# The decoder's steps: biases kept in PSUM, three full products, and four matmuls of ones per step

## The chip, the cores and the metric

The kernel runs on one core of a Trainium2 chip. The metric is device time in microseconds (us) of one launch, lower is better. The engines are named as the profile names them: PE (TensorE's matmuls) and PEld (its weight loads), DVE (VectorE), ACT (ScalarE), POOL (GpSimd), SP (SyncE, which issues most DMAs).

## The reference, cut to what matters

The model is a chain of eight residual blocks on x (16 sequences of 64 tokens, 128 features, f32). The first is a recurrent decoder with attention; a mixture of experts (MoE) follows it, then a perceiver, a quantised MLP, six transformer layers, an MoE, a block and an MoE. Only the decoder and the seam to the first MoE are touched. For each of the 16 sequences the decoder computes, with its input row x normalised:

```
def step(carry, x):
    h, stopped = carry
    stop = jnp.logical_or(stopped, jnp.mean(x) == 0)
    logits = jnp.concatenate([x, h]) @ W_attn.T + b_attn
    aw = jax.nn.softmax(logits)
    applied = aw @ enc
    comb = jax.nn.relu(jnp.concatenate([x, applied]) @ W_comb.T + b_comb)
    h_new = jnp.tanh(comb @ W_ih.T + b_ih + h @ W_hh.T + b_hh)
    out = h_new @ W_out.T + b_out
    ...
```

The 64 steps depend on each other through h, which is 128 features by 16 sequences. Everything that hangs on x alone can be computed for all steps before.

## The kernel before, in words

The decoder is `decoder()`, called as the first of `STAGES`. It has three parts.

The part before the steps normalises x (`norm_half`), transposes it and the context to features (`to_features`), and computes for all steps at once what depends on x: XL, the attention logits of x with biases and mask (`wax2`), XC, minus the combined product with its bias (`wcx`), HX, the state's share of that (`wih`), and E2, the contexts times `wca`, each in SBUF.

The steps are written out in order (`manual_schedule`). In step t TensorE adds to the PSUM tile lg the product of `wah2` with h; ACT takes the exponential into bd (two sequences lie in one block of 128 partitions, so bd has 16 columns); `su` is the sum over a block by a matmul with ones, DVE takes its reciprocal r; `cb` is the context product, 8 blocks of 2 columns; DVE multiplies cb with r and takes the maximum with XC, which is the relu, into co; `hh` collects `whh` times h and `wih` times co; ACT takes tanh into H. lg and hh of the next step begin with a matmul of the identity with XL or HX, a copy into PSUM. `mm4` splits a product into four of 32 output rows each; with f32 every matmul runs as two passes, so `mm4` shows as 8 records and a full product as 2. A list `todo` (`exact_zero`) holds small DVE operations that test exactly whether the mean of a normalised row is zero; some are emitted at the end of each step.

The part after the steps builds `keep` (one until a row has stopped) with a matmul of `tri`, multiplies H with `wout`, adds the bias, masks, adds x, and reduces the reciprocals to their extremes (`watch`), which the end of the kernel checks. Then `moe("m0", ...)` begins, whose operations are ordered by a planner (`_Plan`): each has an engine, an assumed duration and its dependences. The planner also places `fill`: matmuls of ones in bf16 (`units`, 128x512) into a PSUM buffer that nobody reads.

All weights of the first stages are loaded at the start on SP's queue: x, the constants, the context, w0 (the decoder's), then m0 in 8 parts, m0_bd, w1 in 4 parts, wd. All matmuls but the transposes and those of other helpers have line 296 (`mm`) in the profile, so they are told apart by the names of their tiles.

Of the kernel before, what the change touches and what calls it, by code (L numbers as in the profile page):

```python
# [27 lines left out]
NEG = -1e30  # L28
# [14 lines left out]
def _cols(v):  # L43

    return v.reshape(-1, 128).T
# [60 lines left out]
def _layout(i):  # L106
# [7 lines left out]
    arrays["x"] = i["x"].reshape(NTOK, D)  # L114
    arrays["ctx"] = i["ctx_1024"].reshape(NTOK, D)
# [4 lines left out]
    for name, m in (("km_s", i["mask_BxS_bf0"]), ("km_c", i["mask_BxS2_bf0"])):  # L120
# [8 lines left out]
        ("wax", p["W_attn"][:, :D].T),  # L129
        ("wah", p["W_attn"][:, D:].T),  # L130
        ("wcx", p["W_comb"][:, :D].T),
        ("wca", p["W_comb"][:, D:].T),
# [3 lines left out]
        ("bcomb", _cols(p["b_comb"])),  # L136
        ("bih", _cols(p["b_ih"])),
        ("bhh", _cols(p["b_hh"])),
        ("battn", battn),
        ("wah2", np.tile(p["W_attn"][:, D:].T, (1, 2))),  # L140
        ("wax2", np.tile(p["W_attn"][:, :D].T, (1, 2))),
        ("battn2", np.tile(_cols2(p["b_attn"]), (2, 1))),
        ("bout", _rep(p["b_out"])),
# [81 lines left out]
class _Net:  # L225
    def __init__(self, ctx, tc, ins, at):
        self.tc, self.nc, self.ins, self.at = tc, tc.nc, ins, at
        self.const = ctx.enter_context(tc.tile_pool(name="const", bufs=1))
        self.wts = ctx.enter_context(tc.tile_pool(name="wts", bufs=1))
        self.xres = ctx.enter_context(tc.tile_pool(name="xres", bufs=2))  # L230
        self.small = ctx.enter_context(tc.tile_pool(name="small", bufs=2))
        self.n = 0
        nc = self.nc
        self.load_consts()
        self.x = self.xres.tile([128, NT, D], F32, tag="x", name="x_in")
        nc.sync.dma_start(out=self.x, in_=ins["x"].rearrange("(i p) d -> p i d", p=128))
# [18 lines left out]
    def load_consts(self):  # L255
# [6 lines left out]
        nc.sync.dma_start(out=self.ctx, in_=self.ins["ctx"].rearrange("(i p) d -> p i d", p=128))  # L262
# [1026 lines left out]
class _Fast(_Net):  # L1289
# [5 lines left out]
    def __init__(self, ctx, tc, ins, at):  # L1295
# [7 lines left out]
        rows = ins["x"].rearrange("(i p) d -> p i d", p=128)  # L1303
        for h in range(2):
            nc.sync.dma_start(out=self.x[:, h * 4:(h + 1) * 4, :], in_=rows[:, h * 4:(h + 1) * 4, :])

    def load_rest(self, first):
# [7 lines left out]
        nc.sync.dma_start(out=c[:, :cut], in_=src[:, :cut])  # L1315
        self.ctx = self.const.tile([128, NT, D], F32, tag="ctx", name="ctx_tok")
        nc.sync.dma_start(out=self.ctx, in_=self.ins["ctx"].rearrange("(i p) d -> p i d", p=128))
        self.w0 = self.load("w0", "w0", parts=2, pool=first)
# [15 lines left out]
    def mm4(self, out, lhsT, rhs, start=True, stop=True):  # L1334

        for k in range(4):
            rows = slice(32 * k, 32 * k + 32)
            self.mm(out[rows, :], lhsT[:, rows], rhs, start, stop)

    def watch(self, k, r):  # L1340

        nc = self.nc
        nc.vector.tensor_reduce(self.extremes[:, 0, k:k + 1], r, AX.X, ALU.max)
        nc.vector.tensor_reduce(self.extremes[:, 1, k:k + 1], r, AX.X, ALU.min)
# [23 lines left out]

    def load(self, name, tag, parts=1, layout=None, pool=None, bufs=None):
        if tag in ("moe", "moe_b2"):  # L1370
            pool = self.moew
        elif tag == "wd":
            pool = self.wide
        return super().load(name, tag, parts, layout, pool, bufs)
# [3 lines left out]
    def norm_half(self, x, h, out):  # L1378
# [7 lines left out]
        v, r = self.s([128, 4], "lh_v", 4), self.s([128, 4], "lh_r", 4)  # L1386
        nc.vector.tensor_scalar(v, mv[:, :, 1], EPS, None, ALU.add)
        nc.gpsimd.tensor_tensor(r, v, self.minus_half[:, 0:4], ALU.pow)
        nb = self.s([128, 4], "lh_nb", 4)
        nc.vector.scalar_tensor_tensor(nb, mv[:, :, 0], -1.0, r, ALU.mult, ALU.mult)  # L1390
        for k in range(4):
            if k % 2:
                nc.vector.tensor_scalar(
                    out[:, k, :], x[:, h * 4 + k, :], r[:, k:k + 1], nb[:, k:k + 1], ALU.mult, ALU.add)
            else:
                nc.scalar.activation(
                    out[:, k, :], x[:, h * 4 + k, :], AF.Identity, bias=nb[:, k:k + 1], scale=r[:, k:k + 1])
# [112 lines left out]
    def decoder(self):  # L1510
        nc, tc = self.nc, self.tc
        w = self.w0
        x = self.x
        with ExitStack() as st:
            pool = st.enter_context(tc.tile_pool(name="d_sb", bufs=1))
            full = lambda tag: self.tile(pool, [128, B, T], tag)
            H, lnT, XL, XC, HX, RR = (full(k) for k in ("H", "lnT", "XL", "XC", "HX", "RR"))
            E2 = self.tile(pool, [128, NT, D], "E2")
            keep, zero = self.tile(pool, [128, NT], "keep"), self.tile(pool, [128, NT], "zero")
            ones = self.tile(pool, [128, 128], "ones")  # L1520
            nc.gpsimd.memset(ones, 1.0)
            bsum, lbias = self.tile(pool, [128, 1], "bsum"), self.tile(pool, [128, B], "lbias")
            todo = self.exact_zero(pool, x, zero)
            with tc.tile_pool(name="d_ps", bufs=4, space=PSUM) as ps, tc.manual_schedule(engines=None):
                ln = self.tile(pool, [128, NT, D], "ln")
                flat = lambda a, h: a[:, h * 8:(h + 1) * 8, :].rearrange("p b t -> p (b t)")
                ctxT = full("ctxT")
                for h in range(2):
                    self.norm_half(x, h, ln[:, h * 4:(h + 1) * 4, :])
                self.to_features(ps, self.ctx, lambda h, t: nc.vector.tensor_copy(flat(ctxT, h), t))  # L1530
                self.to_features(ps, ln, lambda h, t: nc.scalar.copy(flat(lnT, h), t))

                nc.vector.tensor_scalar(lbias, self.c("half16"), -NEG, NEG, ALU.mult, ALU.add)
                nc.vector.tensor_scalar(lbias, lbias, w("battn2"), None, ALU.add)
                nc.vector.tensor_tensor(bsum, w("bih"), w("bhh"), ALU.add)
                for h in range(2):
                    t = self.tile(ps, [128, 512], "pj")
                    self.mm(t, w("wcx"), flat(lnT, h))
                    nc.vector.tensor_scalar(flat(XC, h), t, w("bcomb"), -1.0, ALU.add, ALU.mult)
                for h in range(2):  # L1540
                    t = self.tile(ps, [128, 512], "pj")
                    self.mm(t, w("wax2"), flat(lnT, h))
                    nc.vector.tensor_tensor(
                        XL[:, h * 8:(h + 1) * 8, :], t.rearrange("p (b t) -> p b t", t=T),
                        lbias[:, h * 8:(h + 1) * 8].unsqueeze(2).to_broadcast([128, 8, T]), ALU.add)
                for h in range(2):
                    t = self.tile(ps, [128, 512], "pj")
                    self.mm(t, w("wih"), flat(XC, h))
                    nc.scalar.activation(flat(HX, h), t, AF.Identity, bias=bsum, scale=-1.0)
                for h in range(2):  # L1550
                    t = self.tile(ps, [128, 4, 128], "pj")
                    for k in range(4):
                        i = h * 4 + k
                        self.mm(t[:, k, :], ctxT[:, 2 * i:2 * i + 2, :].rearrange("p b t -> p (b t)"), w("wca"))
                    self.evac(h, E2[:, h * 4:(h + 1) * 4, :], t)

            with tc.tile_pool(name="d_rs", bufs=2) as rp, tc.tile_pool(name="d_rps", bufs=2, space=PSUM) as ps, \
                    tc.manual_schedule(engines=None):
                for t in range(T):
                    h = w("cond") if t == 0 else H[:, :, t - 1]  # L1560
                    su, cb = (self.tile(ps, [128, 16], k) for k in ("su", "cb"))
                    if t == 0:
                        lg, hh = (self.tile(ps, [128, 16], k) for k in ("lg", "hh"))
                    if t == 0:
                        self.mm(lg, self.ident, XL[:, :, t], True, False)
                    self.mm4(lg, w("wah2"), h, False, True)
                    bd = self.tile(rp, [128, 16], "bd")
                    nc.scalar.activation(bd, lg, AF.Exp)  # L1568
                    if t == 0:
                        self.mm(hh, self.ident, HX[:, :, t], True, False)  # L1570
                    self.mm4(hh, w("whh"), h, False, False)
                    self.mm4(su, ones, bd)
                    r = RR[:, :, t]
                    nc.vector.reciprocal(r, su)
                    for c in range(NT):
                        self.mm4(cb[:, 2 * c:2 * c + 2], E2[:, c, :], bd[:, 2 * c:2 * c + 2])
                    if t < T - 1:
                        lg = self.tile(ps, [128, 16], "lg")
                        self.mm(lg, self.ident, XL[:, :, t + 1], True, False)
                    co = self.tile(rp, [128, 16], "co")  # L1580
# [951 lines left out]
```

## Time and profile before

| | |
|---|---|
| median of the runs shown | 1666.67 us (1665.7, 1666.67, 1673.75) |
| profiled execution: time, span | 1675.33 us, 1673.1 us |
| mean granted clock of TensorE | 0.904 |
| PE busy, PEld busy | 1501.8 us (90%), 1085.0 us (65%) |
| DVE, ACT, POOL busy | 779.8, 536.2, 185.6 us |
| decoder's first matmul of a step, its last tanh ends | 20.4 us, 225.1 us |
| granted clock from 28.25 to 225.1 us | 0.50 |
| first 128x512 matmul of the MoE | 239.2 us |

The ends of matmuls are modelled, so busy time of PE does not tell how much of the array works; the granted clock is what the throttle allowed, 1 being full speed. A row of the timeline gives start and length in us, the engine, the line, the operation, the tile written and those read, the shape, the number of records merged, and in brackets the idle time of the engine before it and what ended it.

### The profile page before, as it was taken

How to read it: one execution, taken by the hardware profiler on the slowest of the kernel's cores; microseconds unless marked ns; L12 is line 12 of the kernel's file. 1: busy time of each engine (PE TensorE's matmuls, PEld its weight loads, DVE VectorE, ACT ScalarE, POOL GpSimd, SP SyncE). 2: the span in 40 equal slices, each digit the busy share in tenths (PEclk: the TensorE clock that was granted, in tenths of full speed). 3: DMA queues.
4: the chain of work that ended last, by engine and by line, in shares of the span. 5: the costliest groups of instructions: out<-in, count | busy, mean ns of one | idle time of the engine just before them, and what ended most of it. 6: DMA issues, size and time to landing. Idle time of an engine off the chain costs nothing.

```text
span 1673.1 us, 51674 instructions
## 1 busy us (share of the span) xinstructions
PE 1501.8 (90%) x23514; PEld 1085.0 (65%) x23514; DVE 779.8 (47%) x2457; ACT 536.2 (32%) x885; POOL 185.6 (11%) x227
## 2 busy tenths in 40 slices
PE   6999989999995699889888989898999899999997
PEld 5888866665774256566655656555576677776665
DVE  3435351226435476565665656565311544345112
ACT  1111134433331123334342433334433233332431
POOL 0000010001000041222221222122000101001000
PEclk7555569999998789999999999999999999999998
DMA  6000000000000050100000000000300200000000
GB/s 223 4 4 5 4 2 1 0 1 2 3 2 10 0 189 17 30 12 12 26 21 16 13 20 12 21 2 2 139 2 1 103 3 2 3 3 1 1 1 16
DMA packets 14354, 38.74 MB, mean 23 GB/s; under 512 B 1682, under 2 KB 6674, under 8 KB 14125
## 3 DMA queue, kind: packets, MB, share of 16 engines
q1 hardware_dynamic: 14125, 35.34, 6.2%
q8 instruction: 186, 3.05, 0.8%
q14 instruction: 43, 0.35, 0.1%
HBM read 34.81 MB, written 0.52 MB: 21 GB/s over the span
## 4 chain that ended last, share of the span: by engine, by line
PE 82%; DVE 11%; ACT 3%; issue 2%; DMA 1%; POOL 0%; SPq 0%; ACTq 0%; DVEq 0%
PE pj L296 42%; PE y L296 11%; PE O L296 9%; PE S L296 6%; PE cb L296 3%; PE hh L296 3%; PE lg L296 3%; DVE qx L2371 2%; PE pj L1926 1%; DVE u L2321 1%; ACT P L2449 1%; PE su L296 1%; PE pj L2262 1%; ACT bd L1568 1%; DVE nq L2209 1%
## 5 line engine op out<-in xcount | busy, mean ns | idle before, releaser
L296 PEld LDWEIGHTS y<-m_sb,H 128*128 128x128 f32 x1568 | 188.7, 192 | 57.3 <-issue 35.6
L296 PE MATMUL y<-m_sb,H 128*128 128x128 f32 x1568 | 193.5, 276 | 16.9 <-DVE x L1732 9.8
L296 PE MATMUL pj<-xT,m_sb 128*128 128x512 f32 x392 | 182.3, 594 | 0.0
L2215 POOL TENSOR_TENSOR nq<-nq,minus_half 128x2 f32<-128x2 f32 x120 | 85.1, 714 | 605.2 <-DVE nq L2212 571.7
L2403 ACT ACTIVATE P<-S 128x1024 f32<-128x1024 f32 x96 | 98.0, 1021 | 116.9 <-PE S L296 116.9
L1708 ACT ACTIVATE H<-pj,m_sb 128x512 f32<-128x512 f32 x128 | 87.5, 687 | 132.7 <-PE pj L296 132.4
L1732 DVE SCALAR_TENSOR_TENSOR x<-y,cw,x 128x128 f32<-128x128 f32 x128 | 39.0, 346 | 186.8 <-PE y L296 186.8
L296 PEld LDWEIGHTS pj<-xT,m_sb 128*128 128x128 f32 x392 | 68.6, 191 | 57.4 <-issue 56.9
L2245 ACT ACTIVATE xn<-x,nq 128x128 f32<-128x128 f32 x100 | 48.4, 492 | 160.1 <-DVE nq L2218 150.3
L2321 DVE TENSOR_TENSOR u<-pj,consts_sb 128x512 f32<-128x512 f32 x96 | 66.3, 691 | 42.6 <-PE pj L296 42.4
L1838 DVE COPY QKV<-pj 128x512 f32<-128x512 f32 x56 | 38.7, 691 | 71.5 <-PE pj L296 71.4
L1708 ACT ACTIVATE H<-pj,b1g,m_sb 128x512 f32<-128x512 f32 x64 | 49.6, 778 | 58.5 <-PE pj L296 55.8
L296 PE MATMUL cb<-bd,E 128*32 128x2 f32 x4096 | 65.4, 192 | 3.2 <-issue 3.1
L296 PEld LDWEIGHTS cb<-bd,E 128*32 128x32 f32 x4096 | 62.8, 156 | 3.6 <-issue 3.2
L296 PE MATMUL pj<-xT,w_sb 128*128 128x512 f32 x128 | 63.1, 610 | 0.9 <-ACT G L2056 0.5
L296 PE MATMUL pj<-xT,l_f 128*128 128x512 f32 x96 | 51.3, 627 | 11.7 <-ACT P L2449 11.5
L296 PE MATMUL pj<-units 128*128 128x512 bf16 x195 | 57.9, 409 | 4.2 <-DVE x L2077 1.9
L1732 DVE SCALAR_TENSOR_TENSOR acc<-y,cw,acc 128x128 f32<-128x128 f32 x64 | 19.5, 346 | 86.5 <-PE y L296 86.5
L1584 ACT ACTIVATE H<-hh 128x16 f32<-128x16 f32 x64 | 12.9, 202 | 138.9 <-PE hh L296 138.9
L296 PE MATMUL pj<-xT,l_s 128*128 128x512 f32 x96 | 52.5, 663 | 5.5 <-DVE u L2321 2.8
L296 PEld LDWEIGHTS O<-Vs,P 128*64 128x64 f32 x1536 | 49.7, 140 | 10.8 <-issue 8.9
L296 PE MATMUL O<-Vs,P 128*64 128x18 f32 x1536 | 53.6, 214 | 3.1 <-DVE On L2416 3.0
(363 smaller groups left out, 2704.3 us busy)
## 6 DMA issues: line engine op xcount, KB each, us to landing
w_sb<-in_w SPq DMA_DIRECT2D x7, 681.5 KB, 8.3
m_sb<-in_m SPq DMA_DIRECT2D x8, 515.0 KB, 7.0
m_sb<-in_m SPq DMA_DIRECT2D x8, 514.5 KB, 6.0
m_sb<-in_m SPq DMA_DIRECT2D x7, 565.5 KB, 9.5
l_f<-in_l SPq DMA_DIRECT2D x6, 578.5 KB, 3.7
l_a<-in_l SPq DMA_DIRECT2D x6, 387.0 KB, 3.2
l_s<-in_l SPq DMA_DIRECT2D x6, 384.0 KB, 3.2
w_sb<-in_w SPq DMA_DIRECT2D x4, 512.5 KB, 11.8
```

The source lines that it names most:

```text
L296: self.nc.tensor.matmul(out, lhsT=lhsT, rhs=rhs, start=start, stop=stop, **kw)
L1568: nc.scalar.activation(bd, lg, AF.Exp)
L1708: nc.scalar.activation(a[:, c, :], ups[c].slot[1], act, bias=b, scale=g)
L1732: nc.vector.scalar_tensor_tensor(acc[:, k, :], src, g, x0[:, i, :] if first else acc[:, k, :], ALU.mult, ALU.add)
L1838: e(o, i.rearrange("p (b t) -> p b t", t=T) if len(o.shape) == 3 else i)
L1926: t = plan.op("PE", 700, lambda t, On=On: [nc.tensor.transpose(t[:, i * 128:(i + 1) * 128], On.slot[1][:, i * 128:(i + 1) * 128], self.ide ...
L2209: nc.vector.bn_stats(out=t[:, i, 0:6], in_=xk[:, i, :])
L2215: return lambda t: nc.gpsimd.tensor_tensor(t[:, :, b], t[:, :, a], self.minus_half[:, 0:2], ALU.pow)
L2245: nc.scalar.activation(o, xk[:, i, :], AF.Identity, bias=f[1], scale=f[0])
L2321: us.append(plan.op("DVE", 690, lambda u, t=t, k=k, table=table: nc.vector.tensor_tensor(view(u[:, k, :]), view(t.slot[1]), self.c(table). ...
L2371: nc.vector.tensor_scalar(o, r, m, None, ALU.mult)
L2403: P = plan.op("ACT", 1030, lambda P, S=S: nc.scalar.activation(P.rearrange("p (g c) -> p g c", g=4), S.slot[1][:, :, 0:256], AF.Exp, scale ...
```

## The change

The diff changes how the decoder starts, steps and ends.

Biases and logits: the PSUM banks lg and hh now hold all 64 steps (two banks each, 32 steps of 16 columns). Matmuls of the identity with broadcast biases fill them at the start, and the products of x are added into the banks in eight portions of 8 steps, logits(k) and states(k), portion 0 before or in step 0, portion t in steps 1 to 7. XL, HX and their identity matmuls per step are gone. states(k) uses `nwih`, minus `wih`.

The step: `wah2`, `whh` and `wih` are full products instead of `mm4`. bd has a second column of zeros per sequence, so cb has 4 columns per block, and one tensor_tensor_scan (multiply, then maximum) replaces multiply and maximum; the reciprocal is written beside XC. `fill` puts matmuls of ones into the idle one of the two su banks: one behind `whh`, one behind cb, two behind `wih`; in steps 1 to 7 logits(t) and states(t) stand in the place of two of them.

Loads: x and ctx come in another layout (one row of 4 KB a partition), ctx and the constants on ACT's queue; m0, m0_bd, w1 and wd are loaded in 14 portions in every third step from step 2 (`load_later`), each behind a copy on POOL that waits for that step's state.

The end: `keep` and `base` (x plus the masked bias) are made in steps 58 to 62, `watch` in steps 31, 59 and 63, and the output product becomes four quarters in the MoE's plan (`decoder_end`).

```diff
+    def load_later(self, name, tag, parts=1, pool=None):
...
+            def begin(gate, a=a, b=min(n, a + step)):
+                nc.gpsimd.tensor_copy(t[:, a:a + 1], gate[:rows])
+                nc.sync.dma_start(out=t[:, a:b], in_=src[:, a:b])
+
+            self.later.append(begin)
...
+            lgs, hhs, sus, cbs = ([self.tile(ps, [128, 512], f"{k}{i}") for i in range(2)]
+                                  for k in ("lg", "hh", "su", "cb"))
...
+            known = dict(start=False, stop=True, skip_group_check=True)
+            for k in range(2):
+                self.mm(lgs[k], self.ident, lbias.unsqueeze(1).to_broadcast([128, 32, B]))
+                self.mm(hhs[k], self.ident, bsum.unsqueeze(2).to_broadcast([128, 32, B]))
...
+            def logits(k):
+                self.mm(sums(lgs, k), w("wax2"), lnT[:, :, 8 * k:8 * k + 8].rearrange("p b t -> p t b"), **known)
+
+            def states(k):
+                self.mm(sums(hhs, k), nwih, XC[:, 8 * k:8 * k + 8, :, 1], **known)
...
-                    if t == 0:
-                        self.mm(lg, self.ident, XL[:, :, t], True, False)
-                    self.mm4(lg, w("wah2"), h, False, True)
-                    bd = self.tile(rp, [128, 16], "bd")
-                    nc.scalar.activation(bd, lg, AF.Exp)
-                    if t == 0:
-                        self.mm(hh, self.ident, HX[:, :, t], True, False)
-                    self.mm4(hh, w("whh"), h, False, False)
-                    self.mm4(su, ones, bd)
-                    r = RR[:, :, t]
-                    nc.vector.reciprocal(r, su)
-                    for c in range(NT):
-                        self.mm4(cb[:, 2 * c:2 * c + 2], E2[:, c, :], bd[:, 2 * c:2 * c + 2])
-                    if t < T - 1:
-                        lg = self.tile(ps, [128, 16], "lg")
-                        self.mm(lg, self.ident, XL[:, :, t + 1], True, False)
-                    co = self.tile(rp, [128, 16], "co")
-                    nc.vector.tensor_tensor(co, cb, r, ALU.mult)
-                    nc.vector.tensor_tensor(co, co, XC[:, :, t], ALU.max)
-                    self.mm4(hh, w("wih"), co, False, True)
-                    nc.scalar.activation(H[:, :, t], hh, AF.Tanh)
-                    if t < T - 1:
-                        hh = self.tile(ps, [128, 16], "hh")
-                        self.mm(hh, self.ident, HX[:, :, t + 1], True, False)
-                    for _ in range(-(-len(todo) // (T - t))):
+            for t in range(T):
+                h = w("cond") if t == 0 else H[:, :, t - 1]
+                lg, hh = (k[t // 32][:, (t % 32) * B:(t % 32 + 1) * B] for k in (lgs, hhs))
+                su, cb, bd = sus[t % 2], cbs[t % 2], bds[t % 2]
+                idle = sus[(t + 1) % 2]
+                self.mm(lg, w("wah2"), h, **known)
+                nc.scalar.activation(bd[:, :, 1], lg, AF.Exp)
+                if t > 0:
+                    self.mm(hh, w("whh"), h, **known)
+                self.fill(idle, 1)
+                self.mm4(su[:, :B], ones, bd[:, :, 1])
+                nc.vector.reciprocal(XC[:, t, :, 0], su[:, :B])
+                for c in range(NT):
+                    self.mm4(cb[:, 4 * c:4 * c + 4], E2[:, c, :],
+                             bd[:, 2 * c:2 * c + 2, :].rearrange("p b k -> p (b k)"))
+                if t == 0:
+                    states(0)
+                    self.mm(hh, w("whh"), h, **known)
+                elif t < 8:
+                    logits(t)
+                else:
+                    self.fill(idle, 1)
+                co = self.tile(rp, [128, B, 2], "co")
+                nc.vector.tensor_tensor_scan(
+                    co.rearrange("p b k -> p (b k)"), cb[:, :2 * B], XC[:, t, :, :].rearrange("p b k -> p (b k)"),
+                    0.0, ALU.mult, ALU.max)
+                self.mm(hh, w("wih"), co[:, :, 1], **known)
+                nc.scalar.activation(H[:, :, t], hh, AF.Tanh)
+                if 0 < t < 8:
+                    states(t)
+                self.fill(idle, 1 if 0 < t < 8 else 2)
+                if t % 3 == 2 and self.later:
+                    self.later.pop(0)(H[:, 0, t:t + 1])
+                if todo:
+                    for _ in range(-(-len(todo) // (T - 6 - t))):
                         todo.pop(0)()
...
+                elif t == T - 6:
+                    self.mm(su[:, 32:32 + NT], self.c("tri"), zero)
+                    nc.vector.tensor_scalar(keep, su[:, 32:32 + NT], 0.5, None, ALU.is_lt)
...
+                for k, (a, b) in enumerate(((0, 32), (32, 60), (60, T))):
+                    if t == b - 1:
+                        self.watch(3 + k, XC[:, a:b, :, 0])
```

In the MoE the normalisation of x and the operation that starts its output now wait for the four quarters:

```diff
+            ends = self.decoder_end("pj") if name == "m0" else [None] * 4
...
-                xTs.append(self.half_norm(half(x0, h), (None, None), copy, "tp"))
+                xTs.append(self.half_norm(half(x0, h), ends[2 * h:2 * h + 2], copy, "tp"))
```

## The prediction

> **What bounds the kernel now.** The page first, for where the decoder lies and at which clock it runs.
>
> ```profile
> PE   6999989999995699889888989898999899999997
> PEclk7555569999998789999999999999999999999998
> ...
> PE 82%; DVE 11%; ACT 3%; issue 2%; DMA 1%; POOL 0%; SPq 0%; ACTq 0%; DVEq 0%
> ```
>
> A slice is 42 us. In slices 2 to 5 TensorE is busy at 90% and more, yet at half clock. The stretches of that part say the same in us (columns: length, then busy time of PE, PEld, DVE, ACT, POOL, granted clock, DMA share and GB/s):
>
> ```profile
> 20.40:25.10 4.70, 4.31 (x177) 3.85 (x177) 1.67 (x7) 0.57 (x3) 0.00 (x0) 0.75 0.99 276
> 25.10:28.25 3.15, 0.02 (x1) 0.00 (x0) 0.00 (x0) 0.00 (x0) 0.00 (x0) 0.50 0.89 335
> 28.25:225.10 196.85, 179.34 (x6223) 160.44 (x6223) 82.89 (x367) 24.33 (x127) 0.00 (x0) 0.50 0.02 5
> 225.10:239.20 14.10, 12.48 (x53) 8.00 (x54) 9.49 (x44) 2.96 (x9) 4.83 (x6) 0.67 0.00 1
> ```
>
> The 64 steps last from 20.4 to 225.1 us: 204.7 us, among them a stall of 3.15 us in step 1 while the bulk loads fill the DMA, and about 2.2 us in the last step, where two reductions of 1.2 us stand in DVE's queue between the reciprocal and the maximum. Then one step in the timeline (start, length, engine, line, operation, out<-in):
>
> ```profile
> 208.15 0.32 PE L296 MATMUL lg<-H,w_sb 128*32 128x16 f32 x8
> ...
> 208.60 0.18 ACT L1568 ACTIVATE bd<-lg 128x16 f32<-128x16 f32 x1 [0.65 <-PE lg L296]
> ...
> 208.84 0.31 PE L296 MATMUL su<-bd,ones 128*32 128x16 f32 x8 [0.24 <-ACT bd L1568]
> ...
> 208.96 1.01 PE L296 MATMUL cb<-bd,E 128*32 128x2 f32 x64
> ...
> 209.91 0.61 PE L296 MATMUL lg<-XL,consts_sb 128*128 128x16 f32 x2
> 210.04 0.18 DVE L1581 TENSOR_TENSOR co<-cb,RR 128x16 f32<-128x16 f32 x1 [0.57 <-PE cb L296]
> ...
> 210.49 0.31 PE L296 MATMUL hh<-co,w_sb 128*32 128x16 f32 x8
> 210.73 0.61 PE L296 MATMUL hh<-HX,consts_sb 128*128 128x16 f32 x2
> 210.87 0.20 ACT L1584 ACTIVATE H<-hh 128x16 f32<-128x16 f32 x1 [2.09 <-PE hh L296]
> ```
>
> lg, Exp, su and cb, two DVE operations, hh, tanh: a chain, 3.11 us from one lg to the next. It is bound by latency, and the latencies on TensorE hang on its clock.
>
> **What the clock follows.** [...] (the granted clock is 1.0 or 0.5, and its changes lie on a grid of 3.413 us)[...]. So I summed per window, over the trace's matmul records, the array-cycles: columns streamed (an f32 pass takes two cycles a column: 512 columns pass in 429 ns at full clock) times the share of the 128x128 array in use. A window has 8192. Of the windows at full clock, those that held it had at least 0.341 and those that lost it at most 0.347; from half clock it stayed lost up to 0.352. One window below decides. A stretch of 7 us without a pause shows that busy time is not what counts:
>
> ```profile
> 569.76 7.17 PE L296 MATMUL pj<-hT,dT 88*128 88x512 f32 x8 [12.40 <-DVE hT L788]
> ```
>
> It uses 88 of 128 rows at half clock, 0.344 of a window, and the clock stays low. (One window came back at 0.319, with tiles of 88 columns.) Counting narrow tiles for 0.3 by their rows alone makes the border clean, at 0.354 to 0.361. The decoder has 0.06.
>
> **The change: its activity.** Per step four matmuls of ones (512 bf16 columns) give 2048 array-cycles, three full products of 16 f32 columns 192, su 64, cb (now 4 columns) 128: 2432. To hold the clock on average a step may last about 2432/8192/0.345 x 3.413 = 2.94 us.
>
> **The step at full clock.** A full product takes 0.39 us warm (step 0, lg<-XL) where four quarters take 0.26; passes follow each other by 0.112 us. lg 0.39, to Exp 0.07, Exp 0.18, to PE 0.05: 0.70. Behind lg, whh's passes issue at 0.25 and 0.36 and a fill at 0.47 that streams 0.213; from a fill to a narrower tile the layers show 0.306 to 0.320 us, so su starts at 0.785, 0.085 late. su to co took 0.87 in step 0 (at full clock): 1.66. One scan replaces two DVE operations of 0.18 and their gap; the trace has scans of 256 elements alone (0.69 us, against 0.42 to 0.44 for a two-tensor operation)[...]: an estimated 0.22 for 32 (0.17 to 0.36, its parent's two operations being the upper end). To PE 0.05, wih 0.39, to ACT 0.07, tanh 0.20, to PE 0.05: **2.64 us**. The second fill (1.55 to 1.76) and the last two (to 2.60) are hidden. In steps 1 to 3 states() writes the PSUM tile that tanh reads and waits for it; lg is queued behind it and a fill on PE: 0.43 more each. All warm, the loop takes 64 x 2.64 + 1.3 + 0.3 = 170.6 us.
>
> **The step at half clock.** A full product 0.61 (0.32 as quarters): Exp ends and su could start at 0.91. whh's passes issue at 0.45 and 0.66, the fill at 0.87, streams 0.427, and the narrower tile follows it by 0.56: su at 1.44, 0.53 lost. su to co 1.20: 2.64; scan and hop: 2.91. The second fill issues at 1.44 + 0.93 + 0.20 = 2.57 and ends at 3.00, 0.09 late. wih 0.61, hops and tanh 0.32: 3.93. The last two fills issue at 3.45 and 3.88 and end at **4.30**, 0.37 late. TensorE's pauses are too short for fills of 0.427. 64 of them less three warm ones: 271 us. Its best window holds four fills, su, cb and wih: 2304, 0.28. Lost once, the clock does not come back in the loop.
>
> **Which of the two.** At 2.64 us a window holds one step and 0.77 us. Placed at worst, these lie between the first fill's end and the second's start (0.69 to 1.55), where only su and cb work: 2432 + 192 = 0.320; with rows counted in part, 0.363. That is on the border. In steps 1 to 3 (3.07 us) the worst is 2432 + 64 = 0.305, with rows 0.326: below in either count, over about 0.7 us of 3.07 of the window's positions, and over some more in the stretch of su and cb. Two or three windows fall there, so I take about two in three that one is low and the clock goes by step 4. Later ones can go at step 31 or 59 (two reductions of about 0.6 in DVE's queue before the reciprocal: up to 0.16 late) or at step 42, where the scheduler has put the reduction of wd_sb behind the scan, just as its load lands.
>
> **The rest.** Loads move: m0, m0_bd, w1, wd (14 DMAs on SP, 14 tiny copies on POOL, which is otherwise idle there) leave the start and come in steps 2 to 41, when the DMA share is 0.02; each is under 0.6 MB, some 1.5 us at the 400 GB/s of the start, all there before the MoE at step 64. The stall of step 1 should go, with them. Below it a fetch behind one load could still cost up to 1.5 us (0 to 5 in all). The start: x and ctx in long rows, ctx and identity from ACT's queue, which is idle until 3.8 us; ctx came at 9.06. But the transposes, four bias products of 128x512 (0.86 each warm, as the removed XL and HX products) and wcx remain, so the loop starts 0.5 earlier (3 earlier to 2 later). The end: keep and base are ready, the output product comes in quarters in the MoE's plan: 14.1 us become about 10.8 (gain 1.5 to 5). DVE's zero test has 3 operations per step in place of up to 3, at most 1.98 us: hidden by cb. Nothing else changes from 239 us on but the windows' phase, +-3.
>
> **Sum.** The profiled execution is the one of 1675.33 (span 1673.1), 0.5% above the median of 1666.67; I take differences off the median. Likeliest, clock lost early: 271 - 204.7 = +66, start -0.5, end -3: +63, **1730 us**; on its own 1712 to 1748 (0.2 us a step is 13).
>
> **Rivals.** (1) The clock holds: 170.6 - 204.7 = -34, start -1, end, projected warm, -5, and up to 5 more if the scan is 0.17: -42, 1624 us. For it: fills fit the pauses to 0.05 us, activity 0.384 on average. Against it: the steps 1 to 3 and the border. It decides at one window of 3.413 us under 0.34 to 0.36. (2) The clock holds until step 31 or 42 and goes: half and half, about 220 us for the loop, 1678 (1645 to 1705). (3) The fills do nothing and half clock was there from the start, because the window before the loop is low: as the forecast, 1735. (4) Instruction fetches stall behind the later loads, 3 us at each of five of them: +15 on (1), 1639, and below the border, so it ends in (2).
>
> **Chances.** Clock lost early, with (3): 0.60. (1) with (4): 0.32. (2): 0.08, half of it slower. What a measurement of this kernel tells from no change is about 0.5%, 8 us. So faster 0.32, same 0.04, slower 0.64. The range has to reach into (1): 1618 to 1748.
>
> **What would show it.** In the profile after: PEclk 5 in slices 2 to 6 or 7, fills of ones of 0.63 us in the loop, lg to lg 4.3 us, su 1.44 behind lg, the fills ahead of su, wih and lg as what they wait behind. Right on the step but wrong on the clock: PEclk 9, lg to lg 2.6, the loop done at 190. Wrong throughout: half clock with steps under 3.3 us, which would mean that fills fit after all, or a clock that comes back within the loop.

## The result and the profile after

The changed kernel takes 1715.33 us (median of 4 executions, 1708.53 to 1719.17) against 1668.95 us before on the same chip (4 executions): a ratio of 1.0271, 95% interval 1.0224 to 1.0319. The forecast was 1730 us, slower. The profiled execution is the one of 1719.17 us, span 1717.4. For several of the kernels below executions differ by the step at which the loop loses its clock, so all of their times or their range are given, and a ratio is formed without those over 1.5% above the kernel's fastest.

The page of the changed kernel: TensorE's busy share and granted clock in 40 slices of 43 us, and the shares of the chain of waits.

```profile
PE   7999999999999669988888888888999899999997
PEclk8555556999999768999999999999999999999999
...
PE 83%; DVE 11%; ACT 2%; issue 2%; DMA 1%; SPq 0%; POOL 0%; DVEq 0%; ACTq 0%
```

Half clock in slices 2 to 6, one slice more than before, and TensorE almost never idle there. The stretches of the decoder (columns: length, busy time of PE, PEld, DVE, ACT, POOL, granted clock, DMA share, GB/s):

```profile
20.40:25.00 4.60, 3.64 (x147) 2.77 (x148) 1.45 (x6) 1.51 (x4) 0.00 (x0) 1.00 0.01 4
25.00:28.40 3.40, 3.11 (x118) 2.59 (x109) 1.31 (x6) 0.38 (x2) 0.00 (x0) 1.00 0.02 5
28.40:46.00 17.60, 17.03 (x337) 14.36 (x337) 4.63 (x20) 1.53 (x8) 0.37 (x2) 0.50 0.21 63
46.00:274.50 228.50, 228.50 (x4685) 161.72 (x4685) 68.77 (x294) 22.17 (x117) 2.20 (x12) 0.50 0.10 29
274.50:288.40 13.90, 11.19 (x52) 8.00 (x51) 8.44 (x42) 3.88 (x8) 4.98 (x6) 0.75 0.01 2
```

The loop enters at full clock, loses it at 28.4 us, in its third step, and gets it back only after the last one. It lasts from 20.34 to 274.5 us, 254 us where it took 204.7. TensorE is busy for 228.50 of 228.50 us: busy throughout, and still at 0.50. One step at half clock in the timeline, to be laid beside the step of before (start, length, engine, line, operation, out<-in, idle time ahead and what ended it):

```profile
166.38 1.01 PE L296 MATMUL su<-units 128*128 128x512 bf16 x2
166.58 0.20 ACT L1667 ACTIVATE H<-hh 128x16 f32<-128x16 f32 x1 [2.69 <-PE hh L296]
...
167.18 0.45 PE L296 MATMUL lg<-H,w_sb 128*128 128x16 f32 x2
...
167.47 0.59 PE L296 MATMUL hh<-H,w_sb 128*128 128x16 f32 x2
167.67 0.18 ACT L1646 ACTIVATE bd<-lg 128x16 f32<-128x16 f32 x1 [0.89 <-PE lg L296]
...
167.90 0.59 PE L296 MATMUL su<-units 128*128 128x512 bf16 x1
168.41 0.20 PEld L296 LDWEIGHTS su<-bd,ones 128*32 128x32 f32 x8 [0.44 <-issue]
...
168.54 1.01 PE L296 MATMUL cb<-bd,E 128*32 128x4 f32 x64
...
169.49 0.61 PE L296 MATMUL su<-units 128*128 128x512 bf16 x1
169.63 0.22 DVE L1663 TENSOR_TENSOR_SCAN co<-cb,XC 128x32 f32<-128x32 f32 x1 [0.57 <-PE cb L296]
...
169.90 0.61 PE L296 MATMUL hh<-co,w_sb 128*128 128x16 f32 x2
```

Two waits behind fills are plain. Tanh ends at 166.78, lg issues at 167.18: 0.35 late, since two fills of 0.427 stand ahead of it. Exp ends at 167.85, su issues at 168.41: 0.51 late, behind one fill. From lg to lg it is 3.98 us (tanh to tanh 3.97 in the median), against 3.11 before.

### The profile page after: what moved, and what is told of

Read it like the earlier page. It is cut to its first block, busy times and chain, and to the rows that moved or that the text cites. A ratio compares the mean times of both kernels' runs of the same rounds, so it can differ in the third digit from the quotient of the medians.

```text
span 1717.4 us, 49317 instructions
## 1 busy us (share of the span) xinstructions
PE 1565.7 (91%) x22375; PEld 1099.6 (64%) x22375; DVE 767.8 (45%) x2401; ACT 535.1 (31%) x884; POOL 188.7 (11%) x244
## 4 chain that ended last, share of the span: by engine, by line
PE 83%; DVE 11%; ACT 2%; issue 2%; DMA 1%; SPq 0%; POOL 0%; DVEq 0%; ACTq 0%
PE pj L296 40%; PE y L296 11%; PE O L296 8%; PE su L296 7%; PE S L296 5%; PE hh L296 3%; PE cb L296 3%; DVE qx L2472 2%; PE lg L296 1%; PE pj L2027 1%; DVE u L2422 1%; ACT P L2550 1%; PE pj L2363 1%; DVE nq L2310 1%; PE tp L296 1%
## 5 line engine op out<-in xcount | busy, mean ns | idle before, releaser
L2316 POOL TENSOR_TENSOR nq<-nq,minus_half 128x2 f32<-128x2 f32 x120 | 85.1, 713 | 609.3 <-DVE nq L2313 575.0
L296 PE MATMUL su<-units 128*128 128x512 bf16 x241 | 132.5, 598 | 0.0
L296 PEld LDWEIGHTS <-units 128*128 128x128 bf16 x480 | 67.7, 151 | 26.3 <-issue 7.8
L1651 DVE RECIPROCAL XC<-su 128x16 f32<-128x16 f32 x64 | 16.5, 258 | 137.9 <-PE su L296 137.9
L296 PE MATMUL cb<-bd,E 128*32 128x4 f32 x4096 | 64.1, 193 | 0.0
L296 PE MATMUL pj<-units 128*128 128x512 bf16 x179 | 54.4, 406 | 3.3 <-DVE x L2178 1.9
## 6 DMA issues: line engine op xcount, KB each, us to landing
m_sb<-in_m SPq DMA_DIRECT2D x7, 565.5 KB, 3.6
```

The source lines that it names most:

```text
L296: self.nc.tensor.matmul(out, lhsT=lhsT, rhs=rhs, start=start, stop=stop, **kw)
L2316: return lambda t: nc.gpsimd.tensor_tensor(t[:, :, b], t[:, :, a], self.minus_half[:, 0:2], ALU.pow)
```

## The experiments

Window sums below are array-cycles by matmul records, as in the prediction, as a share of what a window takes at full clock. The windows are stretches of the grid on which the granted clock changes: in the profile of the change it changes at 28.4, 277.6, 284.4 and 294.7 us, which are 73, 2 and 3 times 3.413 us apart, and all 29 changes in the profile before lie on such a grid to 0.01 us. In the loop, in the profiles of five kernels (the one with quarter products, the one with states() moved, that with a fifth fill, and the two with step 0 filled and four or five fills), one fill in four or five has a weight load but no matmul record; there I took those fills from their loads. The sums are good to a few hundredths at best.

**1. Without the fills**

```
-                self.fill(idle, 1)                         # behind whh
-                else: self.fill(idle, 1)                   # behind cb
-                self.fill(idle, 1 if 0 < t < 8 else 2)     # behind tanh
```

> The changed kernel without the matmuls of ones in the decoder's steps; everything else stays. Theory (the clock was lost at step 2 to 3 and the fills of 0.427 us do not fit the pauses of a cold step): half clock all the way, and the two waits behind fills that the changed kernel's trace shows go, about 0.5 ahead of su and 0.35 ahead of lg; in return lg's own product shows its full 0.65 from issue to Exp where it now takes 0.5. Step 0.65 + 0.18 + 0.05 + up to 0.1 + 1.22 + 0.22 + 0.05 + 0.65 + 0.25 = 3.3 to 3.4 us in place of 3.97, so about 40 us less: 1675 us. Rival A (the full products and the restructured steps are what costs, the fills lie in pauses): step still about 3.9, 1710 to 1715 us. Rival B (the fills hold the clock for the part of the loop where it matters): slower than the changed kernel.

Measured: 1679.41 us (20 executions, 1663.96 to 1684.24), ratio to before 1.006 (1.0039 to 1.0082), half clock from step 1 on, 3.35 us a step. So the fills cost 3.97 - 3.35 = 0.62 us in each step and 36 us in all; rival A and rival B are out.

**2. Quarter products, fills kept**

```
-                self.mm(lg, w("wah2"), h, **known)
+                self.mm4(lg, w("wah2"), h, **known)
...                                                         # whh and wih likewise
```

> The changed kernel with its three products of wah2, whh and wih as four quarter products each again, fills kept. Theory (the cold step waits behind fills): lg as quarters starts later behind the fill, because a narrower tile follows a fill by 0.51 us, and gains nothing; wih gains about 0.15, whh lets the fill ahead of su go 0.05 earlier: 3.75 to 3.85 us a step, 8 to 14 us less, 1701 to 1707 us, half clock as before. Rival (the full product at 0.6 against 0.3 is what makes the step long): 0.3 for lg and 0.3 for wih come back, 3.4 us, 1678 us. The sum of array-cycles is the same, so the clock should be lost at the same place.

Measured: 1699.88 us (1690.37 to 1705.49), 3.73 us a step at half clock. With the fills there, the full products cost 0.24 us a step, not 0.6. The profile is of the execution of 1690.37. The expectation that the clock would go at the same place failed: with the wait of states() still there and the same sum a step, it held full clock until 54.6 us, through windows of 0.25 to 0.34 between 20.5 and 41 us. What ended it (timeline, then the DMA row of the stretch from 45 to 56 us in 40 slices):

```profile
51.30 0.42 PE L296 MATMUL cb<-bd,E 128*32 128x4 f32 x31
...
53.45 0.44 PE L296 MATMUL cb<-bd,E 128*32 128x4 f32 x33 [1.72 <-issue]
```

```profile
DMA  0002000000000079589993200000000000200000
```

TensorE stands for 1.72 us in the middle of cb, with nothing to wait for that the profile shows. The row shows one of the later loads (565.5 KB, from 48.8 us), which is over at 51.2 us, just before the stop; the last 2 of that group is a packet of the instruction queue (q8 on the profile's page) at 51.23 us, and no load moves in the stop itself. The window from 51.2 us fell to about 0.1 and the clock was gone. What such a packet has to do with the stop is taken up under 11 and 12.

**3. The restructured steps alone** (no fills, quarter products; start, loads and end as in the change)

> The restructured steps alone: the changed kernel without the fills of the loop and with wah2, whh and wih as quarter products. Theory: half clock throughout; against the kernel without fills (3.35 us a step) lg and wih lose 0.3 each of the path but su can't start before whh's passes are out: 2.80 to 2.95 us a step against 3.11 before. Loop about 187 us with steps 1 to 3 0.4 longer, against 204.7 before: about 1650 us, faster than before by 1%. Then full products cost about 0.45 us a step and fills 0.62. Rival (the restructured steps themselves cost, by the scan, the wait of states() or the later loads): 3.1 us or more, 1668 us or slower.

Measured: 1651.98 us (1646.56 to 1655.29), ratio 0.9894 (0.9859 to 0.9928), 2.79 us a step, at half clock from 22.8 us, the end of the first step, on. With 1, 2 and the change this makes a square:

| half clock | quarter products | full products |
|---|---|---|
| no fills | 1652.0 us, 2.79 a step | 1679.4 us, 3.35 a step |
| four fills | 1699.9 us, 3.73 a step (one execution at full clock until 54.6 us) | 1715.3 us, 3.97 a step |

So the kernel with its steps rewritten, and with the new start, loads and end, gains 17 us; fills and full products on top of that cost 63 when the clock is not held.

**4. states() moved ahead of su in steps 1 to 7**

```
-                self.fill(idle, 1)
+                if 0 < t < 8: states(t)
+                else: self.fill(idle, 1)
...
-                if 0 < t < 8:
-                    states(t)
-                self.fill(idle, 1 if 0 < t < 8 else 2)
+                self.fill(idle, 2)
```

> The changed kernel with the products of states() in steps 1 to 7 put where the first fill stands (behind whh), and that fill put behind tanh: same work, same number of fills, but lg no longer stands behind a product that waits for tanh. Theory of the clock by array-cycles: steps 1 to 3 shrink from 3.28 us to 2.65, the lowest window rises from 0.305 to 0.320 by array area (0.363 with rows counted in part). If area alone decides with a border of 0.34 to 0.35, the clock is still lost within some ten steps, since the phase between step and window walks: about 1700 to 1715 us. If rows count in part, it holds: about 170 us for the loop in place of 253, 1625 to 1632 us. Rival (the wait of states() is what loses the clock, whatever the border): it holds, 1625 to 1632 us.

Measured: 1721.59, 1684.02, 1719.16 and 1726.69 us. Three of four executions are as slow as the change; in the profiled one the clock goes at 24.4 us, at the end of step 0's window (0.295). There TensorE stands for 0.9 us, because Exp is queued behind an activation of 1.12 us on ScalarE. Moving states() is not enough; a second hole lies ahead of it.

**5. The same with four more fills in step 0**

```
-                else: self.fill(idle, 1)
+                else: self.fill(idle, 5 if t == 0 else 1)
```

> The same as the kernel with states() moved and step 0 filled, but with the change's own four fills a step. Its lowest window at full clock is 0.320 by array area. Theory by area (border between 0.33 and 0.35): the clock goes in the first ten steps or so in most executions, and four fills don't bring it back: 1690 to 1720 us, single executions lower where the phase between steps and windows is lucky. If four a step are enough and only the wait of states() and the idle of step 0 lost the clock: 1630 to 1640 us.

Measured: 15 executions from 1666.76 to 1711.49 us, median 1679.63, ratio 1.004 (1.0014 to 1.0066). The profiled one (1701.75) keeps the clock through steps 1 to 11 at 2.61 to 2.81 us, in windows from 0.34 up, and loses it in the window from 52.1 us (0.298), when a step took 3.45. What made that step long is a stop in cb, with a later load under way:

```profile
54.18 0.65 PE L296 MATMUL cb<-bd,E 128*32 128x4 f32 x55
55.28 0.25 PE L296 MATMUL cb<-bd,E 128*32 128x4 f32 x9 [0.45 <-issue]
```

Without it the fill behind cb would have stood in the same window, some 0.06 of it, and the product wih too: an estimated 0.37 in place of 0.298. So here it was most likely the stop that cost the clock, and whether four fills would hold it where nothing stops TensorE is not shown. It held far longer than the first steps, so the expectation by array area was too strict on time, yet no execution comes near the 1637 us of the kernel that holds it throughout (8).

**6. step 0 filled, states() left where the change has it**

> The changed kernel with four more fills in step 0 and nothing else; states() stays behind tanh. Theory (the wait of states() in steps 1 to 3, 0.43 us each, takes a window below the border): the clock is lost at steps 1 to 3 as in the changed kernel, 1705 to 1718 us. Rival (the idle of step 0 lost it, the wait is harmless): as the kernel with states() moved and step 0 filled, 1667 to 1711 us with a median near 1680.

Measured: 1714.62 us (1702.54 to 1724.31), ratio 1.0264 (1.0194 to 1.0333), clock lost at 31.1 us, in the window from 27.6 us (0.306). It differs from 5 in the place of states() alone, and no stop lies ahead of its loss; so the wait of states() can lose the clock by itself. It need not: 2, in its profiled execution, came through the same wait at full clock. In the changed kernel it looks like this (timeline, from step 1 to step 2):

```profile
26.08 0.20 ACT L1667 ACTIVATE H<-hh 128x16 f32<-128x16 f32 x1 [1.75 <-PE hh L296]
...
26.33 0.50 PE L296 MATMUL hh<-XC,nwih 128*128 128x128 f32 x2 [0.29 <-ACT H L1667]
26.66 0.38 PE L296 MATMUL su<-units 128*128 128x512 bf16 x1
...
26.88 0.29 PE L296 MATMUL lg<-H,w_sb 128*128 128x16 f32 x2
```

The product of states() waits for tanh, the fill and lg stand behind it, and lg comes 0.55 us later than it could.

**7. states() moved, and a fifth fill**

```
-                else: self.fill(idle, 1)                   # behind cb, from step 8
+                self.fill(idle, 0 if t == 0 else 1 if t < 8 else 2)
```

> As the kernel with states() moved, and a fifth fill in the pause between cb and wih from step 8 on, where a warm step has room for two. Theory: the lowest window at full clock has (2944 + 192)/8192 = 0.38, above every border seen, so the clock holds through all 64 steps; the fifth fill lies in a pause of 0.5 us and costs nothing warm. Step 2.65, loop about 171 us against 253, 82 us less, and the output product starts at full clock: 1625 to 1635 us, faster than the kernel before. Rival (the clock can't be held by such fills because narrow matmuls of su and cb leave it idle 0.87 us in each step): lost within a few steps, and five fills make the cold step 0.4 us longer: about 1740 us.

Measured: 1660.42, 1655.02, 1632.97 and 1633.01 us, ratio, without the 1660.42, 0.9839 (0.9764 to 0.9915). The profiled execution (1660.42) lost the clock in step 0's window (0.276), ran 14 steps at half clock, 4.18 to 4.6 us each, and got it back at 85.1 us by itself; from there on most steps take 2.62.

**8. Five fills, and step 0 filled**

> As the kernel with five fills, and four more fills in step 0 ahead of su, where TensorE idles 0.9 us until Exp (the window of step 0 was 0.276 in the profile of the kernel with five fills and lost the clock there). Theory: the clock then holds from the first step in nearly every execution, step 2.62 us, loop 170 us, 1630 to 1636 us with less spread than 1633 to 1660. Rival (the loss at the start comes from another cause, such as an instruction fetch behind a load): spread as before, 1633 to 1660, median about 1645.

Measured: 1636.56 us (1640.06, 1629.20, 1635.53, 1637.60), ratio 0.9797 (0.9762 to 0.9832): faster than both kernels. The clock row of its page, and the start of a step:

```profile
PEclk9999999999997699899998999999999999999999
```

```profile
52.74 0.39 PE L296 MATMUL lg<-H,w_sb 128*128 128x16 f32 x2
...
53.18 0.18 ACT L1646 ACTIVATE bd<-lg 128x16 f32<-128x16 f32 x1 [0.48 <-PE lg L296]
53.21 0.38 PE L296 MATMUL su<-units 128*128 128x512 bf16 x1
53.52 0.16 PEld L296 LDWEIGHTS su<-bd,ones 128*32 128x32 f32 x8 [0.23 <-ACT bd L1646]
...
53.60 0.73 PE L296 MATMUL cb<-bd,E 128*32 128x4 f32 x64
```

Full clock in all 64 steps, 2.62 us in the median (2.94 in steps 1 to 7, which carry states() and logits(), and up to 3.27 where TensorE stops in cb), and su only some 0.1 late behind its fill: at 0.213 us a fill fits where one of 0.427 did not. The lowest window of the loop has 0.36. The loop's last tanh starts at 195.3 us.

**9. Half the rows.** Kernel 8 with each fill of the loop over 64 of 128 rows, by a copy of `fill` that the steps alone call:

```
-            self.mm(t, self.units[:, :128], self.units)
+            self.mm(t, self.units[:64, :128], self.units[:64, :])
```

> As the kernel with five fills and step 0 filled, but each matmul of ones over 64 of the 128 rows (contraction over 64 partitions), 512 columns as before: TensorE is busy as long, the array half as full. Theory (array-cycles count): 5 x 256 + 384 = 1664 a step, 0.26 of a window at 2.62 us a step: lost in the first steps and never back: step about 4.2 us, 1725 to 1740 us. Rival (the time in which TensorE is busy counts, or the columns streamed): holds, 1630 to 1640 us.

**10. Half the columns.** Kernel 8 with each fill of the loop into 64 of 128 columns, likewise:

```
-            self.mm(t, self.units[:, :128], self.units)
+            self.mm(t[:64, :], self.units[:, :64], self.units)
```

> The kernel with five fills and step 0 filled, but each matmul of ones into 64 of the 128 columns of the array (64 output partitions), all 128 rows and 512 columns streamed. Theory (array-cycles count): 1664 a step as with 64 rows, lost in the first steps, half clock for the rest; a switch of tile shape at every fill as there: 1770 to 1795 us. If rows count alone (all 128 are in use here, 64 there), the clock holds: 1630 to 1640 us; if rows count in part, it may hold for some steps: in between.

Measured: 64 rows 1789.18 us (1784.0 to 1790.98), ratio 1.0721 (1.0687 to 1.0756), 5.04 us a step; 64 columns 1659.27 us (20 executions, 1652.37 to 1668.98), ratio 0.996 (0.9937 to 0.9983), 3.05 us a step. The clock rows, first that of 64 rows, then that of 64 columns:

```profile
PEclk8555555699999986998999999999999999999999
```

```profile
PEclk9999999999997689999999999999999999999999
```

With 64 columns the clock holds through the whole loop, although every window of it has only 0.20 to 0.29 by array area; with 64 rows it is lost at 26.9 us, after two steps, though TensorE streamed for 0.43 of the window before, no less than the 0.42 of windows that held with 64 columns. So the area of the array in use does not tell here whether the clock is kept, and streaming time alone hardly does: the two windows lie only 0.01 apart, but all four executions with 64 rows are as slow, and all 20 with 64 columns as fast, as their profiled one. What fits both is streaming time times the share of rows in use, with the columns left out. Counted so (four quarter products as one), the windows of the loop with 64 columns have 0.35 and more. Quarter products leave the count open, though. If each of them counts by its rows in full, as leaving the columns out would have it, the loops of all fourteen profiles fit better: full clock was lost in windows of up to 0.41 and held from 0.39 up. With four counted as one it was lost up to 0.33 and held from 0.25 up. The layers have products of 64 columns too (S, O and some of pj, tiles of 32*64 and 128*64). Counted by their rows in full, the kernel before loses the clock in a window of 0.507 and holds it in one of 0.386; counted as half each, it loses it up to 0.347 and holds it from 0.341 (windows from 12 us on). So there the count fits only with half for each, where the fills of this run count in full; no run varied that. The steps are longer than in kernel 8, where a fill and a full product have the same tile shape: with 64 columns, at full clock, a full product follows a fill by 0.31 us, where it follows a fill of full size by 0.22. Of the 0.44 us by which a step is longer, 0.19 lie ahead of lg, 0.11 ahead of su and 0.10 ahead of wih.

**11. The later loads in halves**, one a step from step 2 on, in kernel 8:

> The kernel with five fills and step 0 filled, with the later loads in halves of about 0.28 MB, one at the end of every step from step 2 on, in place of one of 0.56 MB after every third. In the profile of the kernel with five fills six of the steps that follow a load are 0.35 to 0.65 us longer: TensorE stands in the middle of cb and waits for nothing that the profile shows, while the load fills the DMA. Theory (an instruction fetch stands behind the load's packets): a load half as long delays a fetch by half at most; those excesses shrink from 3.1 us in sum to 1 us or less and the clock is never lost: 1627 to 1634 us with less spread. Rival (what delays is that any load is under way): as many steps lengthen or more, 1636 us or over.

**12. All later loads at the end of step 2**, in kernel 8:

> The kernel with five fills and step 0 filled, with all the later loads issued at the end of step 2, one behind the other: 7.2 MB, about 18 us of full DMA at 400 GB/s. Theory (instruction fetches stand behind the loads, and one long stall takes a window below the border): one or more stalls of 2 to 4 us in steps 3 to 10, as the 3.15 us of the kernel before in its step 1; the clock goes to half and comes back by the five fills after some ten steps: 1645 to 1665 us. Rival (fetches are not held up by loads): 1630 to 1640 us as with spread loads, or less.

Measured: halves 1640.78 us (6 executions, 1630.72 to 1649.84), ratio 0.9827 (0.9777 to 0.9876), no better than kernel 8, so the idea that a load half as long delays half as much falls. Burst: 1657.25, 1681.1, 1668.28 and 1636.58 us. The timeline of the halves and, below it, of the burst:

```profile
63.20 0.62 PE L296 MATMUL cb<-bd,E 128*32 128x4 f32 x51
64.89 0.30 PE L296 MATMUL cb<-bd,E 128*32 128x4 f32 x13 [1.07 <-issue]
```

```profile
40.15 0.45 PE L296 MATMUL cb<-bd,E 128*32 128x4 f32 x33
...
42.73 0.60 PE L296 MATMUL cb<-bd,E 128*32 128x4 f32 x31 [2.12 <-issue]
```

In both TensorE stops in the middle of cb for 1 to 2 us under the loads, a window falls to 0.28 (halves) or 0.23 (burst), and the clock goes; after 12 and 9 steps it is back. That stops of 1.07 and 2.12 us cost the clock here is shown. But a stop does not need a load under way: the six longer steps of which the expectation of 11 speaks are those of kernel 8 (0.35 to 0.65 us longer), and in three of them no load was under way. The burst shows it best. Its last load is in by 53 us, and at 187 us it still stops (timeline, then the DMA row of the stretch from 184 to 190 us in 40 slices of 0.15 us):

```profile
186.95 0.69 PE L296 MATMUL cb<-bd,E 128*32 128x4 f32 x59
188.06 0.23 PE L296 MATMUL cb<-bd,E 128*32 128x4 f32 x5 [0.43 <-issue]
```

```profile
DMA  0000000005000000000000000000000000400000
```

All that moves there are two packets of the instruction queue (16 KB each). Over the fourteen profiles there are 50 places where two neighbouring matmuls of cb start more than 0.15 us apart, in place of about 0.01. At every one TensorE goes on 2.2 to 2.9 us after a packet of that queue (q8) starts, while those packets come 4.5 us apart in the median. 29 of the 50 had no load within 3 us before; there the two matmuls start 0.60 us apart at most. Where they start 0.62 us or more apart, a load was under way or had ended less than 3 us before, and in 2 the packet came as soon as the load was through. So the stops go with packets of that queue, and the long ones with a packet beside or behind a load. That the packets cause them was not shown: no run varied them.

## Why the prediction was right, point by point

**The direction and its cause hold.** The clock was lost in the third step and never came back in the loop; the prediction named steps 1 to 3, by the wait that states() puts ahead of lg (6), and no return at half clock (its best window there is 0.29, the prediction had 0.28). It gave this 0.60, and the range that it stated, 1618 to 1748 us, took in the rival of a held clock too, so that the measured time lies in it says little. That the clock went in the first steps was in part luck: 2, with the same wait and the same sum, kept it through them in its profiled execution. The rival (1624 us) is a kernel that the change is not: it takes states() moved, a fifth fill and a filled step 0 to make it (8, 1637 us), and the step that it was worked out with, 2.64 us, measured 2.62.

**The step at half clock was mis-sized: 4.30 forecast, 3.97 measured.** Of its terms, su behind the fill (0.53, measured 0.51), lg behind two fills (0.37, measured 0.35), su to co (1.20, measured 1.21) and the scan (0.22, measured 0.22) stand. The term that failed is lg itself: 0.61 + 0.07 from its issue to Exp, taken from a product that issues with TensorE idle. Standing ready behind a fill it issues late but takes 0.49: its two passes issue 0.07 us apart, where in the kernel without fills (1) they are 0.23 apart and lg takes 0.64. That is 0.19; why the passes lie closer behind a fill was not shown. (wih, let go just as its fill ends, takes 0.65.) The second fill makes wih late by nothing where 0.09 was reckoned, since co is ready at 169.85 and wih issues at 169.90. The rest is in tanh's hops. Over 60 steps this is 20 us; steps 3 to 8, longer than the others (4.64 and 4.17), give 2 of them back, and the loop came to 254 us in place of 271.

**The rest of the sum.** The start: first tanh at 23.45 us against 23.14, no gain where 0.5 was reckoned. The stall of 3.15 us did go: the second tanh follows the first by 2.63 us in place of 6.39. In the last step of before the prediction misread a term: that step took 4.70 us where the others take 3.11, so the two reductions cost it 1.6 us and not 2.2. The sum does not hang on it, since the whole loop of 204.7 us was taken off.

The end: 14.1 us were to become 10.8 and took 13.9, so -3 forecast and next to nothing measured, and what follows lost 3 us more. From the last tanh to the first activation of the MoE's 128x512 products it is 16.0 us against 15.4, and their first 64 take 116.0 against 113.0. The quarters of the output product brought the clock up at once, at 277.6 us (0.442 in the window before), and then TensorE waited for the norm:

```profile
284.01 0.20 PEld L2363 LDWEIGHTS tp<-consts_sb,xn 128*128 128x128 f32 x2 [3.10 <-ACT xn L2346]
```

so the window from 281.0 us had 0.17, the clock went again at 284.4 and came back at 294.7, where before it rose at 234.4 and stayed. The step that failed is that the end would shorten by what is taken out of it: its length hung on where the clock rose. Later stages gave 9 us back (last activation of the MoE line at 1696.2 against 1652.4, +43.8, from +52.9 at the first 64), with 90 us at half clock from 290 us to 1650 us against 102 before. The prediction had +-3 for that phase; the two profiles differ by more, and half clock explains about 6 of it. What the other 3 are I did not follow.

**The border was too sharp, and wrong in kind.** The windows that lost the clock in the loop had 0.331 (the change), 0.306 (6) and 0.298 (5); held ones there go down to 0.325 (the change, from 21.6 us), 0.309 (6, from 24.2 us) and 0.25 (2, from 23.9 us). So between 0.25 and 0.35 this count does not tell, and the border of 0.341 to 0.347 is not one. Nor does it tell when the clock comes back: in 7, 11 and 12 it came back after a window of 0.33 and had stayed low after windows of 0.35. And the share of the array's columns that a fill uses made no difference to the clock (10: full clock with 64 as with 128): the prediction took area, since the tiles of 88 that stayed cold use 88 of the rows, and set aside the one window that contradicted it, at 0.319 with tiles of 88 columns. With rows alone that window has 0.457 and is no exception. The fills, of 128 x 128, count the same either way, which is why the forecast did not suffer.

**Of the rivals**, the stalls of (4) are real (that fetches make them was not shown), though not at each load: 1 to 2 us of stop where a load falls badly (2, 11, 12), against 3 us reckoned. In kernel 8 they make a step up to 0.65 us longer, with loads and without. In the changed kernel the clock is gone before the first load.

## What to carry to other kernels

Work that is added to keep a clock has to be sized for the state in which the clock is lost: here a fill takes 0.213 us at full clock and fits its pause, and 0.427 at half clock and does not, so fills that hold the clock make a kernel 33 us faster (8, with more of them and states() moved), and fills that lose it one 46 us slower. Count activity in the worst window of the clock's grid (3.413 us in these profiles) that can lie over the loop, the first step and the steps with extra work included, and leave a margin for stops that no count foresees: four fills a step (5, windows from 0.34) lost the clock to a stop of 0.45 us; five, with the first step filled (8, windows from 0.36), came through stops of that size and lost it to those of 1.07 and 2.12 us (11, 12). And judge a rewritten loop apart from what is added to it: without fills and full products the change was worth 1%, at half clock.

## What the runs showed of the hardware that was not expected

- A matmul of 512 bf16 columns into 64 of the array's 128 columns kept the clock as one into 128 did; one over 64 of its 128 rows did not (1659 us and full clock against 1789 us and half clock, with five of them a step).
- At half clock the loop got its clock back without a change in its work: with five fills (up to 0.35 in its windows) it came back after 14, 12 and 9 steps, each time after a window of 0.33; with four (up to 0.32) in no profile.
- At half clock a full product that stood ready behind a fill (lg) took 0.49 us from issue to the next engine; one that was let go with TensorE idle (lg in 1), or just as a fill ended (wih), took 0.64 and 0.65.
- TensorE stopped in the middle of a run of small matmuls with no load under way, for 0.43 us in 12 at 187 us, and each of the 50 stops found ended 2.2 to 2.9 us after a packet of the instruction queue started. Beside or behind a load of 0.28 to 0.57 MB three stops took 1.07, 1.72 and 2.12 us (11, 2, 12); halving the loads did not do away with them.
